# Masked attention over a sparse graph: attention's steps begin earlier, and one tile is transposed onto another in PSUM

## The chip, the cores and the metric

The kernel runs on one core of a Trainium2 chip. The metric is the time of one execution on the device in microseconds (us); three runs of the kernel before gave 635.58, 635.72 and 637.35, median 635.72. The engines go by the profile's names: PE (TensorE, matrix products; PEld is its weight load), DVE (VectorE), ACT (ScalarE), POOL (GpSimd) and SP (SyncE, which here only issues DMAs). [...]

## The reference

With x of 2708 x 1024 and adj of 2708 x 2708, which holds a 1 with a chance of 0.0014771 and a 0 otherwise (some four edges in a row):

```python
h = jnp.maximum(_layernorm(x, axis=-1), 0.0)
q = h @ W_q.T + b_q
k = h @ W_k.T + b_k
v = h @ W_v.T + b_v
z = scale * (q @ k.T)                     # scale = 1 / sqrt(1024)
spare_z = z * adj
spare_z = jnp.where(spare_z == 0.0, -10000.0, spare_z)
out = softmax(spare_z, axis=1) @ v
x = x + relu(out)
```

## The kernel before

**The algebra.** M = scale W_q^T W_k is formed once. q stands for h M (so that a score is q of a row times h of its neighbour), and the weighted sum of neighbours' h rows is multiplied by W_v at the end. Only rows that adj marks are ever read: the kernel searches adj for the edges, sorts the rows by their number of edges, and works on tiles of 128 rows of like number. Tile t has K[t] slots; for the tiles that matter here K is 3, 3, 4, 5, 5 for tiles 6, 5, 4, 3, 2, then 7 for tile 21 (the second part of the longest rows), 8 for tile 0, 1 for tile 20, 2 for 7, 3 for 17, 5 for 13, 3 for 18. Tile 20 has no scores. This is also attention's order.

**Units.** The products run in 20 units of two tiles each. Units 0 to 9 make q of tiles (0, 1) to (18, 19); units 10 to 19 make the outputs, in attention's order: (6, 5), (4, 3), (2, 0), (20, 7), (17, 13) and so on. Each unit multiplies a 2 x 2 arrangement of blocks in seven block products instead of eight (Strassen's way, Winograd's form): the first tile's halves are a11 and a12, the second tile's are a21 and a22, and four sums are formed of them by `blocks`:

s1 = a21 + a22, s2 = s1 - a11, s3 = a11 - a21, s4 = a12 - s2.

`multiply` issues the products in this order: Y s2, X a12, Z s4, Y s3, then of the next unit X a11 and Z s1 (`opened`, called by `between`), then Y a22. Each is four matrix products of 128 x 128 by 128 x 512, which are eight instructions in the profile (line 1010). X, Z and Y are banks of PSUM; the next unit's banks take over those that have been read. Between the products stand the points `after(0)` to `after(6)`: `after(i)` says what the other engines do at that place. The results leave by c11, c12, c22 and c21: c12 (line 1094, DVE) after Z s4; c22 (line 1091, DVE) after Y s3; c21 (line 1099, ACT) after Y a22. Bank Y is added into again by Y a22 after c22 has read it. In units 4 and 5 (`EARLY <= ta < EARLY + 4`) and in the output units ACT copies Y for c22 first; in the other q units DVE reads Y itself.

**Operands.** Rows of a tile are turned by PE (`half_turned`, line 415: four transposes into one bank of PSUM) and copied out by ACT (line 718), or, where a tile was finished early enough ("faced"), they are stored in quarters and turned by DVE (line 705). `upper` makes a11 and a12, `lower` makes a22 and the sums. In most units `upper` is at point 0 and `lower` at point 2 of the unit before; where `turn` is set (units 0 and 3) they are at points 3 to 5.

**Attention** is a generator, `stream`, of small steps: a score is one DVE instruction over 128 x 1024 (line 863, `junk`), counted as 1.3 us; the weights of a tile count 0.6; each further slot's sum is one DVE instruction (line 923, `u`), counted as 1.3. `advance(share)` at each point takes out steps until `share` us are spent; `share` is 20.9/7 (21.5/7 in the last units), less 2.3/7 for each faced row of the next unit. DVE's order is the written one from start to end (`manual_schedule`); the order of ACT and POOL is written in units 0 to 3 and chosen by the compiler's scheduler after that, as PE's and SP's is. A tile's scores need `pq`, its q rows in sorted order: for tiles under 8 a gather from q_dram, for the others a plain load from q_late (line 833, issued by POOL), which unit (t / 2) has stored through SP (line 1084). They need `g`, the neighbours' rows, gathered by POOL into eleven buffers (line 610).

**Before attention** come the search for edges (`found`, line 389), the list of each row's neighbours (`listed`, lines 402 to 408), `counts` (lines 661 to 669), `sort` (lines 678 to 689, two small products on PE), the scatter of the table into DRAM (`put`, line 626), its `reload` (line 638), and the clearing of the buffers g (line 1262). The list `steps_at` says at which (unit, point) each runs, and `steps_ahead` what runs ahead of the rest of a point: `"i21"` finds tile number 21 of the search, `"j21"` lists it, `"c0"` counts and `"o0"` sorts the first half of the rows, `"w0-7"` scatters, `"b0"` reloads.

**Places that the change touches**: `blocks` (line 718 and after), `steps_at` and `steps_ahead`, `opened`, the loop over units with `share`, the memsets (line 1262), `advance`, and the place where `load_rows` fetches the rows of the unit after next (line 612 for q's).

Of the kernel before, what the change touches and what calls it, by code (L numbers as in the profile page):

```python
# [10 lines left out]
FT = mybir.dt.float32  # L11
# [4 lines left out]
ALU = mybir.AluOpType  # L16
AX = mybir.AxisListType

P = 128
# [46 lines left out]
def tile_preln_masked_attention(  # L66
# [12 lines left out]
    nc = tc.nc  # L79
# [28 lines left out]
    psum = ctx.enter_context(tc.tile_pool(name="psum", bufs=4, space=bass.MemoryType.PSUM))  # L108
# [13 lines left out]
    ident = const.tile([P, P], FT, name="ident")  # L122
# [70 lines left out]
    first = const.tile([P, PARTS, 8], FT, name="first")  # L193
# [216 lines left out]
    def half_turned(xt, s):  # L410
# [4 lines left out]
            nc.tensor.transpose(pt[:, c, :], xt[:, k * P:(k + 1) * P], ident)  # L415
        return pt

    def turned(xt, name):

        hT = work.tile([P, D], FT, tag="hT", name=f"T_{name}", bufs=2).rearrange("p (c q) -> p c q", q=P)  # L420
        for s in range(DC // 4):
            nc.scalar.copy(hT[:, s * 4:(s + 1) * 4, :], half_turned(xt, s))
        return hT
# [7 lines left out]
    tp = low.enter_context(tc.tile_pool(name="tp", bufs=1, side="left", reuse_waits="tile"))  # L431
# [14 lines left out]
    with tc.tile_pool(name="w", bufs=1, side="left") as wp:  # L446
# [73 lines left out]
        if True:  # L520
# [13 lines left out]
            for o in range(DC):  # L534
# [4 lines left out]
                else:  # L539
                    k = o - H  # L540
# [61 lines left out]
    half = low.enter_context(tc.tile_pool(name="half", bufs=1, side="left", reuse_waits="tile"))  # L602
# [11 lines left out]
    rows_of = {}  # L614
    FIRST = EARLY // 2
# [6 lines left out]
    def put(lo, hi):  # L622

        before_them = puts[lo >= EARLY]
        for t, (t0, n) in tiles_of(lo, hi):
            put = nc.gpsimd.indirect_dma_start(  # L626
                out=tab_dram[lo >= EARLY][:, :], out_offset=bass.IndirectOffsetOnAxis(ap=pos_i[:n, t:t + 1], axis=0),
                in_=tab[:n, t, :], in_offset=None)
            for other in before_them:
                tc.declare_no_dep(put.ins, other.ins, reason="rows of a permutation")  # L630
            before_them.append(put)
        return put
# [75 lines left out]
    def is_faced(xt):  # L708
        return any(xt is y for y in faced)

    def blocks(xa, xb, eng=None):


        ops = {}

        def held(name, bank):
            ops[name] = small(name).rearrange("p (c q) -> p c q", q=P)
            nc.scalar.copy(ops[name], bank)

        def put(name, a, b, op, eng=None):  # L720
            ops[name] = small(name).rearrange("p (c q) -> p c q", q=P)
            step = (eng or nc.vector).tensor_tensor(ops[name], a, b, op=op)  # L722
            if eng is None:
                behind.append(step)

        def faced_half(name, xt, s):
            ops[name] = small(name).rearrange("p (c q) -> p c q", q=P)
            faces(ops[name], xt, s * 4, s * 4 + 4)

        def upper():  # L730
            for s, name in enumerate(("a11", "a12")):
                if is_faced(xa):
                    faced_half(name, xa, s)
                else:
                    held(name, half_turned(xa, s))

        def lower():
            if is_faced(xb):
                faced_half("a22", xb, 1)
                faced_half("s3", xb, 0)  # L740
                put("s1", ops["a22"], ops["s3"], ALU.add)
                behind.append(nc.vector.tensor_sub(ops["s3"], ops["a11"], ops["s3"]))
            else:
                held("a22", half_turned(xb, 1))
                a21 = half_turned(xb, 0)
                put("s1", ops["a22"], a21, ALU.add)
                put("s3", ops["a11"], a21, ALU.subtract)
            put("s2", ops["s1"], ops["a11"], ALU.subtract, eng)
            put("s4", ops["a12"], ops["s2"], ALU.subtract, eng)

        return ops, upper, lower

    placed = []

# [8 lines left out]
    def natural_rows(n):  # L763
# [3 lines left out]
    ops_of = {0: blocks(*rows_of.pop(0))}  # L767
# [19 lines left out]
    steps_ahead = {(1, 5): "o1", (3, 6): "o0"}  # L787

    slots, free = [], []

# [217 lines left out]
    def add_block(bank, a, b, last=True):  # L1008
        for c in range(4):
            mm = nc.tensor.matmul(bank, a[:, c, :], b[:, c, :], start=False, stop=(c == 3), skip_group_check=True)  # L1010
        return mm
# [3 lines left out]
    def opened(n):  # L1015

        if n not in banks_of:
            return
        X, Z = banks_of[n]
        ops = ops_of[n][0]  # L1020
        add_block(X, ops["a11"], M[:, 0, 0])
        Y = psum.tile([P, NB], FT, tag="acc", name="psy")
        nc.scalar.copy(Y, X)
        products.append(add_block(Z, ops["s1"], T[:, 0] if units[n][0] == "q" else M[:, 0, 1]))
        p5 = small("p5")
        nc.scalar.copy(p5, Z)
        opened_of[n] = Y, p5
# [203 lines left out]
    for n, unit in enumerate(units):  # L1231
# [5 lines left out]
            nc.sync.dma_start(bp_dram, bp_sb[0:1, :])  # L1237
        turn = n in (0, FIRST - 1)
        share = (20.9 if n < len(units) - 5 else 21.5) / 7
        nxt = units[n + 1] if n + 1 < len(units) else None  # L1240
        if nxt is not None and nxt[0] == "o":
            share -= 2.3 / 7 * len(set(nxt[1:]) & faced_tiles)
# [2 lines left out]
        def after(i):  # L1245
# [4 lines left out]
            if (n, i) == (2, 5):  # L1250
# [5 lines left out]
                owe(7)  # L1256
                rows_of[FIRST + 1] = load_rows(units[FIRST + 1])
                pooled.close()
            if n == FIRST and i in (1, 4, 5):
                for g in slots[:4] if i == 1 else slots[4:6] if i == 4 else slots[6:8]:  # L1260
                    with tc.issue_after(sorted_at[-1].ins):
                        nc.vector.memset(g, 0.0)
            b11, t1, b21, b22 = M[:, 0, 0], M[:, 0, 1], M[:, 1, 0], M[:, 1, 1]
# [24 lines left out]
                marked(EARLY, NT)  # L1288
            if (n, i) == (FIRST + 2, 4):
                nc.vector.tensor_scalar(msq, msq, MLIMIT, None, op0=ALU.is_gt)  # L1290
            if n > FIRST + 1 or n == FIRST + 1 and i > 1:
                advance(share)
            if nxt is not None:

                if i == (3 if n == 0 else 4 if turn else 0):
                    ops_of[n + 1] = blocks(*rows_of[n + 1], nc.gpsimd if n + 1 < FIRST - 1 else None)
                    with tc.issue_after(products[-1].ins) if n + 1 == FIRST else nullcontext():
                        ops_of[n + 1][1]()
                if i == (4 if n == 0 else 5 if turn else 2):
                    ops_of[n + 1][2]()  # L1300
                    rows_of.pop(n + 1)
                    if n == last_q - 1:
                        all_rows()
                if i == 3:
                    banks_of[n + 1] = banks_for(bp_sb)
                if i == 6 and n + 2 < FIRST:
                    natural_rows(n + 2)
                if i == (2 if n == FIRST else 3 if n == last_q else 4) and n + 2 > FIRST and n + 2 < len(units) and n + 2 not in rows_of:
                    while units[n + 2][0] == "o" and not done.issuperset(units[n + 2][1:]):
                        advance(1.0)  # L1310
                    rows_of[n + 2] = load_rows(units[n + 2])
# [259 lines left out]
```

## Time and profile before

| what | value |
|---|---|
| median of three runs | 635.72 us (635.58 to 637.35) |
| the profiled execution's own time | 631.83 us |
| its span, first to last instruction | 630.1 us |
| PE busy | 619.6 us (98%) |
| DVE busy | 523.3 us (83%) |
| ACT busy | 288.4 us (46%) |
| POOL busy | 363.1 us (58%) |
| granted clock of PE, mean | 0.999 |
| DMA | 182.19 MB, mean 289 GB/s |

The times in a row of a timeline are the start from the beginning of the span and the duration, both in us; in brackets stands how long the engine was idle before it and what ended that. In a row of the waits stand the total, the number and the longest. In a row of the chain of waits stand start and duration. In a row of groups stand count, busy time and mean ns of one, then the idle time before them. DVE and ACT instructions overlap by some 0.1 us from one to the next.

### The profile page before, as it was taken

How to read it: one execution, taken by the hardware profiler on the slowest of the kernel's cores; microseconds unless marked ns; L12 is line 12 of the kernel's file. 1: busy time of each engine (PE TensorE's matmuls, PEld its weight loads, DVE VectorE, ACT ScalarE, POOL GpSimd, SP SyncE). 2: the span in 40 equal slices, each digit the busy share in tenths (PEclk: the TensorE clock that was granted, in tenths of full speed). 3: DMA queues.
4: the chain of work that ended last, by engine and by line, in shares of the span. 5: the costliest groups of instructions: out<-in, count | busy, mean ns of one | idle time of the engine just before them, and what ended most of it. 6: DMA issues, size and time to landing. Idle time of an engine off the chain costs nothing.

```text
span 630.1 us, 6067 instructions
## 1 busy us (share of the span) xinstructions
PE 619.6 (98%) x1579; PEld 310.3 (49%) x1579; DVE 523.3 (83%) x1022; ACT 288.4 (46%) x421; POOL 363.1 (58%) x394
## 2 busy tenths in 40 slices
PE   8999999999999999999999998999999999999996
PEld 5777766444444444454454443444444444444442
DVE  5999879997996664887988969999997999988741
ACT  3538985749677563343341333434342323343300
POOL 2649860885778177754561632757667477852241
PEclk9999999999999999999999999999999999999999
DMA  8999997688796439997489998899999999997481
GB/s 330 407 371 326 343 354 294 209 288 326 255 387 241 166 113 319 350 379 236 154 306 325 332 359 265 235 333 346 347 318 324 344 278 305 349 284 194 103 296 71
DMA packets 65088, 182.19 MB, mean 289 GB/s; under 512 B 9959, under 2 KB 20023, under 8 KB 64408
## 3 DMA queue, kind: packets, MB, share of 16 engines
q0 software_dynamic: 26656, 86.02, 43.4%
q1 hardware_dynamic: 31594, 71.53, 32.8%
q10 hardware_dynamic: 6798, 24.20, 9.8%
q8 instruction: 14, 0.23, 0.2%
q14 instruction: 26, 0.21, 0.1%
HBM read 146.70 MB, written 43.36 MB: 302 GB/s over the span
## 4 chain that ended last, share of the span: by engine, by line
PE 56%; DMA 17%; DVE 11%; issue 9%; POOL 4%; ACT 1%; SPq 1%; POOLq 0%; DVEq 0%; ACTq 0%
PE ps L1010 22%; PE psy L1010 15%; PE ps_y L476 7%; DMA out_dram<-y,tab 5%; PE ps_x L476 4%; DMA or<-u_dram 4%; PE ps_z L476 4%; DVE junk L863 4%; PE pt L415 3%; DMA pq<-q_late 2%; DVE u L923 2%; DMA q_late<-q 2%; DMA g<-h_dram,tab 2%; DMA u_dram<-v 1%; DVE a L705 1%
## 5 line engine op out<-in xcount | busy, mean ns | idle before, releaser
L1010 PE MATMUL psy<-wlow,s 128*128 128x512 f32 x320 | 144.0, 592 | 0.0
L1010 PE MATMUL ps<-M,a 128*128 128x512 f32 x320 | 144.0, 593 | 0.0
L610 POOL DMA_INDIRECT g<-h_dram,tab x91 | 110.3, 1212 | 55.8 <-ACT u L912 19.8
L863 DVE SCALAR_TENSOR_TENSOR junk<-g,pq 128x1024 uint8<-128x1024 f32 x90 | 110.0, 1223 | 16.8 <-DMA g<-h_dram,tab 10.2
L1010 PE MATMUL ps<-M,s 128*128 128x512 f32 x240 | 108.0, 592 | 2.2 <-DVE s L722 2.2
L1010 PEld LDWEIGHTS psy<-wlow,s 128*128 128x128 f32 x320 | 59.9, 190 | 72.4 <-issue 70.2
L1010 PEld LDWEIGHTS ps<-M,a 128*128 128x128 f32 x320 | 59.9, 190 | 71.8 <-issue 71.3
L923 DVE SCALAR_TENSOR_TENSOR u<-g,coef,u 128x1024 f32<-128x1024 f32 x66 | 84.6, 1282 | 4.9 <-ACT u L912 3.5
L1010 PEld LDWEIGHTS ps<-M,s 128*128 128x128 f32 x240 | 45.4, 190 | 59.7 <-issue 58.3
L389 DVE FIND_INDEX8 at<-ones,adj 128x8 uint32<-128x685 f32 (+1 forms) x88 | 74.5, 865 | 0.0
L1010 PE MATMUL psy<-wlow,a 128*128 128x512 f32 x160 | 72.0, 593 | 0.1
L368 ACT ACTIVATE sized<-adj 128x2708 uint8<-128x2708 f32 (+1 forms) x22 | 54.3, 2466 | 7.5 <-DMA adj<-in_adj_dram 6.1
L298 POOL TENSOR_TENSOR hsum<-hsum,x 128x256 f32<-128x256 f32 (+1 forms) x56 | 38.7, 728 | 25.4 <-DVE wlow L444 22.0
L1109 POOL DMA_INDIRECT y<-in_x_dram,tab x19 | 32.2, 1696 | 31.4 <-ACT y L1126 22.4
L1010 PEld LDWEIGHTS psy<-wlow,a 128*128 128x128 f32 x160 | 30.3, 190 | 38.7 <-issue 37.3
L944 ACT COPY v<-u 128x1024 f32<-128x1024 f32 x19 | 19.9, 1045 | 48.9 <-DVE u L923 43.5
L808 POOL DMA_INDIRECT out_dram<-y,tab x21 | 27.8, 1325 | 22.0 <-issue 13.6
L1010 PE MATMUL ps<-wlow,s 128*128 128x512 f32 x80 | 36.0, 592 | 0.0
L626 POOL DMA_INDIRECT tab_dram<-tab,pos_i x22 | 21.9, 993 | 20.9 <-DVE pos_i L689 15.4
L912 ACT ACTIVATE u<-g,coef 128x1024 f32<-128x1024 f32 x18 | 20.7, 1148 | 24.2 <-DVE coef L911 24.1
L760 ACT COPY ps<-bp_sb 128x512 f32<-128x512 f32 x42 | 24.6, 595 | 11.0 <-DVE y L1144 10.3
L276 ACT ACTIVATE x<-x,r 128x1024 f32<-128x1024 f32 (+1 forms) x22 | 25.8, 1232 | 5.6 <-POOL r L266 5.6
(251 smaller groups left out, 848.5 us busy)
## 6 DMA issues: line engine op xcount, KB each, us to landing
adj<-in_adj_dram SPq DMA_DIRECT2D x21, 1354.0 KB, 11.2
x<-in_x_dram SPq DMA_DIRECT2D x21, 512.0 KB, 4.2
h_dram<-x ACTq DMA_DIRECT2D x21, 512.0 KB, 8.4
u_dram<-v ACTq DMA_DIRECT2D x19, 512.0 KB, 8.5
or<-u_dram SPq DMA_DIRECT2D x76, 128.0 KB, 9.7
q_late<-q SPq DMA_DIRECT2D x12, 512.0 KB, 9.4
pq<-q_late POOLq DMA_DIRECT2D x12, 512.0 KB, 10.5
M<-in_wv_dram SPq DMA_DIRECT2D x3, 1024.0 KB, 15.4
```

Of the source, the lines that this page charges most:

```text
L276: nc.scalar.activation(xs[i][:n], xs[i][:n], AF.Relu, bias=r[:n, 4, i:i + 1], scale=r[:n, 3, i:i + 1])
L298: small.append(nc.gpsimd.tensor_add(hsum[:n, cols], hsum[:n, cols], xt[:n, cols]))
L368: nc.scalar.activation(sized[:n], a[:n, :, :PW], AF.Abs, accum_out=total[:n, t:t + 1])
L389: nc.vector.max_index(at[:n, k - first_k, g, :], ones[:n, 0:8], a[:n, g, :])
L476: mm = nc.tensor.matmul(bank, a_tile(o + H * a[0], a[1], i), b(o), start=first and o == 0, stop=(o == H - 1), skip_group_check=True)
L610: return nc.gpsimd.indirect_dma_start(out=dst, out_offset=None, in_=src, in_offset=off, bounds_check=N - 1, oob_is_err=False)
L760: nc.scalar.copy(return_[h], row[:, h * NB:(h + 1) * NB])
L808: to = nc.gpsimd.indirect_dma_start(out=out, out_offset=bass.IndirectOffsetOnAxis(ap=ptab.bitcast(U32)[:n, t, SLOTS:SLOTS + 1], axis=0), i ...
L863: chained(lambda: nc.vector.scalar_tensor_tensor(junk, g_of[t][s], 1.0, tq[t], op0=ALU.mult, op1=ALU.mult, accum_out=zall[:, t, s:s + 1]))
L923: chained(lambda: nc.vector.scalar_tensor_tensor(u, g_of[t][s], coef[:, s:s + 1], u, op0=ALU.mult, op1=ALU.add))
L1010: mm = nc.tensor.matmul(bank, a[:, c, :], b[:, c, :], start=False, stop=(c == 3), skip_group_check=True)
L1109: return nc.gpsimd.indirect_dma_start(out=y[:n], out_offset=None, in_=x, in_offset=off, compute_op=ALU.add)
```

## The change

It has five parts.

1. `"j21 c0"` (list and count) moves from point 5 to point 4 of unit 3, and the sort, `"o0"`, from point 6 of unit 3 into `opened`, between unit 4's first two products.
2. The eight memsets of g, which stood at points 1, 4 and 5 of unit 4, all stand at point 1.
3. `advance` begins at point 0 of unit 5, no longer at point 2, and `share` is less by 2.3/7 in unit 9 and by 4.6/7 in unit 10.
4. The q rows for units 7, 8 and 9 are gathered at point 2 of units 5, 6 and 7, no longer at point 4.
5. For units 3 and 5 and after, where the second tile isn't faced, a new step at point 1, `middle`, transposes its upper half (a22) into a bank, from which ACT copies it; at point 2 the lower half (a21) is transposed onto the same bank, so that PE forms s1 = a22 + a21 there and ACT copies s1. DVE makes s2 = s1 - a11, s3 = a22 - s2 and s4, and no longer s1. Units 1, 2 and 4 stay as they were.

```diff
+    def turn_onto(pt, xt, s, first):
+
+        for c in range(4):
+            k = s * 4 + c
+            nc.tensor.matmul(pt[:, c, :], xt[:, k * P:(k + 1) * P], ident, is_transpose=True, start=first and c == 0,
+                             stop=(c == 3), skip_group_check=True)
...
-    def blocks(xa, xb, eng=None):
+    def blocks(xa, xb, eng=None, onto=False):
...
+        half = []
+
+        def middle():
+            if onto and not is_faced(xb):
+                half.append(psum.tile([P, 4, P], FT, tag="tp", name="pt"))
+                turn_onto(half[0], xb, 1, True)
+                held("a22", half[0])
+
         def lower():
             if is_faced(xb):
...
-            else:
+                put("s2", ops["s1"], ops["a11"], ALU.subtract, eng)
+            elif not onto:
                 held("a22", half_turned(xb, 1))
                 a21 = half_turned(xb, 0)
                 put("s1", ops["a22"], a21, ALU.add)
                 put("s3", ops["a11"], a21, ALU.subtract)
-            put("s2", ops["s1"], ops["a11"], ALU.subtract, eng)
+                put("s2", ops["s1"], ops["a11"], ALU.subtract, eng)
+            else:
+                turn_onto(half[0], xb, 0, False)
+                held("s1", half[0])
+                put("s2", ops["s1"], ops["a11"], ALU.subtract)
+                put("s3", ops["a22"], ops["s2"], ALU.subtract)
             put("s4", ops["a12"], ops["s2"], ALU.subtract, eng)
...
-                (3, 1): "i21", (3, 3): "p21", (3, 5): "j21 c0 g0", (3, 6): "w0-7 g1 g2 g3 g4", (4, 4): "b0"}
-    steps_ahead = {(1, 5): "o1", (3, 6): "o0"}
+                (3, 1): "i21", (3, 3): "p21", (3, 4): "j21 c0", (3, 5): "g0", (3, 6): "w0-7 g1 g2 g3 g4", (4, 4): "b0"}
+    steps_ahead = {(1, 5): "o1"}
...
         Y = psum.tile([P, NB], FT, tag="acc", name="psy")
         nc.scalar.copy(Y, X)
+        if n == FIRST:
+            follow("o0")
         products.append(add_block(Z, ops["s1"], T[:, 0] if units[n][0] == "q" else M[:, 0, 1]))
...
+        if n in (last_q, last_q + 1):
+            share -= 2.3 / 7 * (n - last_q + 1)
...
-            if n == FIRST and i in (1, 4, 5):
-                for g in slots[:4] if i == 1 else slots[4:6] if i == 4 else slots[6:8]:
+            if n == FIRST and i == 1:
+                for g in slots[:8]:
                     with tc.issue_after(sorted_at[-1].ins):
                         nc.vector.memset(g, 0.0)
...
-            if n > FIRST + 1 or n == FIRST + 1 and i > 1:
+            if n > FIRST:
                 advance(share)
...
-                    ops_of[n + 1] = blocks(*rows_of[n + 1], nc.gpsimd if n + 1 < FIRST - 1 else None)
+                    ops_of[n + 1] = blocks(*rows_of[n + 1], nc.gpsimd if n + 1 < FIRST - 1 else None, n > 1 and not turn)
...
+                if i == 1 and not turn:
+                    ops_of[n + 1][3]()
...
-                if i == (2 if n == FIRST else 3 if n == last_q else 4) and n + 2 > FIRST and n + 2 < len(units) and n + 2 not in rows_of:
+                if i == (2 if FIRST <= n <= last_q - 2 else 3 if n == last_q else 4) and n + 2 > FIRST and n + 2 < len(units) and n + 2 not in rows_of:
```

Here FIRST is 4 and last_q is 9.

More of the change, by code (lines that the diff above doesn't have):

```diff
@@ L747, in lower @@
                 put("s3", ops["a11"], a21, ALU.subtract)
-            put("s2", ops["s1"], ops["a11"], ALU.subtract, eng)
+                put("s2", ops["s1"], ops["a11"], ALU.subtract, eng)
[4 more added lines that the diff above has]
+                put("s3", ops["a22"], ops["s2"], ALU.subtract)
             put("s4", ops["a12"], ops["s2"], ALU.subtract, eng)
-        return ops, upper, lower
+        return ops, upper, lower, middle
     placed = []
```

## The prediction

> **What bounds the kernel now.** I read the page's head first, then the waits of PE, then PE's timeline where the longest wait lies, then the chain of waits and the timelines of DVE and POOL behind it.
>
> ```profile
> span 630.1 us, 6067 instructions
> PE 619.6 (98%) x1579; PEld 310.3 (49%) x1579; DVE 523.3 (83%) x1022; ACT 288.4 (46%) x421; POOL 363.1 (58%) x394
> ...
> PE ps L1010 <- DVE s L722: 2.2, 1, 2.2
> PE ps_y L511 <- POOL hsum L121: 1.2, 1, 1.2
> PE ps L1010 <- DVE T_alone L705: 0.8, 1, 0.8
> PE ps_x L476 <- DMA wlow<-in_wq_dram: 0.6, 1, 0.6
> ```
>
> TensorE is the bound: busy 619.6 of 630.1 us. All its waits on record come to 4.8 us, and 2.6 of these lie at the start and the end, which the change doesn't touch. No product or transpose is removed, so the most that can be gained is the one wait of 2.2 us. What can be lost has no such limit: the change moves work on DVE, whose order is written out by hand, and PE waits for DVE at some places. Here is the wait:
>
> ```profile
> 360.65 3.60 PE L1010 MATMUL ps<-M,a 128*128 128x512 f32 x8
> 364.08 3.60 PE L1010 MATMUL ps<-M,s 128*128 128x512 f32 x8
> 367.52 3.60 PE L1010 MATMUL psy<-wlow,a 128*128 128x512 f32 x8
> ...
> 384.68 3.60 PE L1010 MATMUL ps<-M,a 128*128 128x512 f32 x8
> 390.44 3.67 PE L1010 MATMUL ps<-M,s 128*128 128x512 f32 x8 [2.16 <-DVE s L722]
> ```
>
> A block of eight rows is 3.43 us (start to start). Unit 9 (tiles 18 and 19, the last of q) ends with the block at 367.52; unit 10 follows, and inside it unit 11's second product (390.44) waited 2.16 us for its operand s1. DVE before that:
>
> ```profile
> 365.73 0.68 DVE L1091 TENSOR_TENSOR q<-psy,p 128x512 f32<-128x512 f32 x1
> 366.33 1.22 DVE L863 SCALAR_TENSOR_TENSOR junk<-g,pq 128x1024 uint8<-128x1024 f32 x1
> ...
> 367.47 1.28 DVE L923 SCALAR_TENSOR_TENSOR u<-g,coef,u 128x1024 f32<-128x1024 f32 x1
> 372.38 1.23 DVE L863 SCALAR_TENSOR_TENSOR junk<-g,pq 128x1024 uint8<-128x1024 f32 x1 [3.64 <-DMA pq<-q_late]
> ...
> 373.65 1.23 DVE L863 SCALAR_TENSOR_TENSOR junk<-g,pq 128x1024 uint8<-128x1024 f32 x1
> ...
> 389.60 0.69 DVE L722 TENSOR_TENSOR s<-a,s 128x512 f32<-128x512 f32 x1
> ```
>
> DVE ran late by itself and then stood 3.64 us for the q rows of attention's tile 17. The chain of waits says where these come from:
>
> ```profile
> 347.73 10.06 DMA q_late<-q
> ...
> 358.32 13.95 DMA pq<-q_late
> ```
>
> q of tile 17 is the last result of unit 8. It is stored when that unit ends (347.73), lands at 357.79, is read back by POOL from 358.32 and is there at 372.27. These two times are set by PE's progress and by DMA, not by how early attention begins.
>
> **The change, part by part.**
>
> *Keys, sort, memsets (unit 3 and 4).*
>
> ```profile
> 208.76 0.28 DVE L402 TENSOR_TENSOR cand<-first,at 128x128 f32<-128x128 f32 x1
> ...
> 205.18 0.69 DVE L1091 TENSOR_TENSOR q<-psy,p 128x512 f32<-128x512 f32 x1 [3.56 <-PE psy L1010]
> ...
> 213.27 0.22 DVE L669 TENSOR_SCALAR tab<-keys 128x128 uint32<-128x128 f32 x1
> 216.48 0.31 DVE L682 COPY sort<-ps_all 128x144 f32<-128x144 f32 x1 [2.99 <-PE ps_all L680]
> ...
> 240.75 1.23 DVE L863 SCALAR_TENSOR_TENSOR junk<-g,pq 128x1024 uint8<-128x1024 f32 x1 [5.17 <-DMA g<-h_dram,tab]
> ...
> L1262 DVE MEMSET g<- 128x1024 f32 x8 | 7.3, 912 | 1.3 <-issue 1.3
> 209.28 3.60 PE L1010 MATMUL ps<-wlow,s 128*128 128x512 f32 x8
> ```
>
> The listing and counting (208.76 to 213.5, 4.7 us) moves one point up, ahead of the addition at 205.18, where DVE stood idle 3.56 us. So unit 4's additions slip by about 1 us; their s1, due on PE at 209.28, is ready near 207.7. The two products of the sort go between two blocks, before 209.28 instead of after 216.15 (two blocks earlier, 6.9 us). The table's scatters, its reload and the first gathers follow on POOL and SP in the same order, so the first score moves from 240.75 to about 233.9. Eight memsets in one row cost (7.3 + 1.3) 8.6 us of DVE, from about 212.2 to 220.8, and unit 5's additions start at 224.7. Nothing of this reaches PE: cost 0; without the 3.56 us of idle time 1 to 3 us would.
>
> *Attention steps.* Each of a unit's seven points (0 to 6) takes 20.9/7 = 2.99 us of steps. After the change unit 5 gives seven points instead of five, and units 9 and 10 lose 2.3 and 4.6 us. I count where the first score of tile 17 falls, since that is the step that waits. The steps ahead of it are 37 scores (tiles 6, 5, 4, 3, 2, 21, 0, 7 with 3, 3, 4, 5, 5, 7, 8, 2 slots) and 30 sums at 1.3, and eight weights at 0.6: 91.9 us. It runs at the first point where more than 91.9 has been given out. Before: 26 points of 2.99 in units 5 to 8 are 77.6, and unit 9 gives 16.3/7 = 2.33 each (its next unit has two faced rows: 20.9 - 4.6), so 91.6 at point 5 and 94.0 at point 6: point 6, as the trace shows (two scores from 372.38, after the addition of 365.73). After: 28 points are 83.6, unit 9 gives (20.9 - 4.6 - 2.3)/7 = 2.0: 91.6 at point 3, 93.6 at point 4. So it moves to **point 4, ahead of the addition c22 of unit 9** (the row at 365.73). That addition reads PE's bank Y in place (only tiles 8 to 11 have it copied by ACT first), and the block of 367.52 adds into the same bank, so PE can't start it before c22 has read. c22 now queues behind two scores that wait for the q rows of tile 17.
>
> With landing time L, c22 ends at L + 3.2: from the landing at 372.27 the second score ended at 374.88, and c22 takes 0.68 more. PE's wait is L + 3.2 - 367.5 = L - 364.3. DVE was there at 368.7 before (372.38 less 3.64); now it has c22 and five additions of 0.68 less ahead, and its steps, 4.6 us more of them by then, began 6.9 sooner: it will be there some 6 us earlier, ahead of L. c22's own input is ready at 360.65. The old wait of 2.16 us goes: between L and s1 stand the 17.9 us of before (372.38 to 390.29) and 2.5 us more (c22, one score, one weights), so s1 is ready at L + 20.4, while PE, late by L - 364.3, wants it at 388.3 + L - 364.3 = L + 24.
>
> What is L? Rows of the store (L1084) and of the read (L833), each least, median, longest, and two single reads:
>
> ```profile
> DMA to landing us min/median/max: 2.6/7.9/12.2
> ...
> DMA to landing us min/median/max: 6.5/10.5/16.4
> ...
> pq<-q_late POOLq DMA_DIRECT2D x1, 512.0 KB, 8.4
> ...
> 352.88 1.49 POOL L610 DMA_INDIRECT g<-h_dram,tab  x1 [0.30 <-issue]
> 358.32 0.57 POOL L833 DMA_DIRECT2D pq<-q_late  x1 [3.95 <-DMA q_late<-q]
> ```
>
> POOL had stood 3.95 us for the store, so the read can't be issued sooner unless the store lands sooner. I keep the store at 10.06 and take the median 10.5 for the read rather than its own 13.95: the gathers that ran up to 352.88 ahead of it are asked for some 6 us sooner and should be further through. L = 358.3 + 10.5 = 368.8; wait 4.5 us. Low end: store 7.9, 0.5 to issue, read 8.4 (that of 380.26, no gather close ahead): L = 364.5, wait 0.2. High end: the longest read, 16.4: L = 374.7, wait 10.4.
>
> [...]
>
> *a21 onto a22 in PSUM.*
>
> ```profile
> L722 DVE TENSOR_TENSOR s<-a,s x26: 691/692/693, 108.0 to 583.9; 128x512 f32<-128x512 f32 x26
> L722 DVE TENSOR_TENSOR s<-a,pt x24: 670/680/689, 106.1 to 555.1; 128x512 f32<-128x512 f32 x24
> ...
> L718 ACT COPY a<-pt x32: 564/590/619, 104.5 to 549.2; 128x512 f32<-128x512 f32 x32
> ...
> 521.24 1.04 PE L415 MATMUL pt<-ident,u 128*128 128x128 f32 x8
> ...
> 522.40 1.04 ACT L944 COPY v<-u 128x1024 f32<-128x1024 f32 x1 [3.72 <-DVE u L923]
> ...
> 526.44 0.57 ACT L718 COPY a<-pt 128x512 f32<-128x512 f32 x1
> ```
>
> It applies to eight units (3, 5 to 9, and the two output units with an untransposed second tile). DVE loses one addition of 0.68 each (5.4 us, none on PE's path but where DVE is late), ACT gains one copy of 0.59 each (it is 46% busy). PE has the same eight transposes, but four come a block earlier, and the last four may not begin before ACT has copied a22 out of that bank. That is a new wait of PE on ACT, with one block (3.43 us) of cover. ACT stands for DVE now and then: at 522.40 it had waited 3.72, and a22's copy ended at 527.0. Were it to stay at that place, PE, which wants it near 521.7, would wait 5.3 us; if ACT takes it before v, nothing. In q's units the copies of the first tile came early enough. I take 0, since the copy is now issued a block sooner, and keep 5.3 as the end.
>
> *q rows sooner.* Six gathers on POOL, some 1.3 us each with their issue, move two blocks up in units 5 to 7; POOL is 58% busy and the score gathers behind them belong to steps that are 6 us ahead: 0. SP gets nothing new. If POOL's order let the gathers of tile 13 past the read of tile 17, that would count to L's high end.
>
> **Sum.** 631.8 (the profiled execution's own time, span 630.1) - 2.16 + 4.5 = 634.2, or +2.3 us. The runs' median is 635.7, 3.9 above the profiled time; I add the difference to it: **638.0 us**, 0.37% slower. About 0.3% (1.9 us) is what a measurement of this kernel can tell from no change.
>
> **Rivals.**
> - *The q rows land in time* (the ending on the other side). With L at 364.5 or less c22 isn't held, and the old wait is gone: -2.2 us, 633.6. For it: the read of 8.4 us, and gathers that leave the queue sooner. Against it: store and read together took 24.5 us and must take under 16.8 (347.73 to 364.5). It decides at L = 366.5, where old and new wait are equal.
> - *ACT's copy of a22 holds PE too*, at the late output units: with the forecast's wait and half of 5.3 on top, +5.0, 640.7. For it: ACT's waits for DVE stand just there. Against it: ACT's order is chosen by readiness, and the copy is ready early.
> - *The wait stays where it was.* If DVE reaches these scores so late, or the order comes out so, that c22 isn't held and s1 is still late: 0, 635.7. Against it: DVE's order in the trace is the written one everywhere I compared.
>
> **How the numbers follow.** Forecast (PE held before the last block of unit 9 by 2.2 to 8 us): 0.50, with times from 635.7 to 641.5. Rows in time: 0.27. ACT's copy: 0.13. No shift: 0.10. Slower by over 0.3%: the part of the forecast with L above 368.4 (0.32) and ACT's (0.12): 0.44. Faster by over 0.3%: nearly all of the second case, 0.24, as its gain is just over that bound. Within: the rest, 0.32. The range from 633.3 to 642.0 reaches from the in-time case to the read of 13.95.
>
> **What would show it.** Right: on DVE the first score of tile 17 stands ahead of unit 9's L1091 addition, with a wait for pq<-q_late; PE waits for that addition before the psy<-wlow,a block near 367.5; no wait for s1 in unit 10; the first score near 234. Wrong: PE without a wait there (L was early), PE waiting for ACT's copies of a22, or the score behind the addition.

## The result, and the profile after

The changed kernel takes 640.3 us (median of ten runs, 637.9 to 648.5) against 636.4 us for the kernel before (median of ten): a ratio of 1.0065, with a 95% interval of 1.0043 to 1.0088. It is slower by about 4 us. The ratios and intervals of this document leave out executions more than 1.5% above the fastest of their kernel, such as the one of 648.5. Its profiled execution has a span of 640.6 us and a time of 642.3. The profiled execution of the kernel before (631.8) is shorter than all its other executions on this chip (634.3 and more in these ten, 633.2 and more in all), so the two spans are 10.5 us apart where the medians differ by 3.9. On a second chip, which comes up below, the kernel before takes 630.9 to 634.5, and which chip the first trace comes from isn't known. The traces are read below for places, and the ratios for sizes.

The head of the page after:

```profile
span 640.6 us, 6061 instructions
PE 624.8 (98%) x1579; PEld 312.2 (49%) x1579; DVE 522.4 (82%) x1014; ACT 294.1 (46%) x429; POOL 365.0 (57%) x394
```

TensorE is busy for 5.2 us more with the same 1579 instructions: some of them ran slower. The rest is waits. What PE waited for, after (line and tile, releaser: total, times, longest):

```profile
PE pt L422 <- ACT a L725: 3.3, 1, 3.3
PE ps L1031 <- ACT ps L781: 2.9, 1, 2.9
PE ps L1031 <- DMA M<-in_wv_dram: 1.6, 1, 1.6
PE ps_y L518 <- POOL hsum L121: 1.2, 1, 1.2
PE ps L1031 <- DVE q L1114: 0.9, 1, 0.9
PE psy L1031 <- DVE q L1114: 0.4, 1, 0.4
```

The old wait for s1 in unit 10 (2.2) and the small one near the end (0.8) are gone. Five new ones have come. The two large ones are for ScalarE, at the transposes of a21 onto a22 and at the copies that open a unit's banks. A unit's operands are made in the unit before: the wait in unit 2 (183.11 below) belongs to the transposes for unit 3, the one in unit 5 (256.30) to those for unit 6. PE's timeline at the four places of interest (start, duration, line, tile, count, idle time and releaser); "..." separates units 2, 5 and 9:

```profile
172.70 0.60 PE L422 MATMUL pt<-ident,x 128*128 128x128 f32 x4
176.57 3.60 PE L1031 MATMUL psy<-wlow,s 128*128 128x512 f32 x8
183.11 5.40 PE L1031 MATMUL ps<-M,a 128*128 128x512 f32 x8 [2.94 <-ACT ps L781]
...
249.36 3.60 PE L1031 MATMUL psy<-wlow,s 128*128 128x512 f32 x8
256.30 1.12 PE L422 MATMUL pt<-ident,qr 128*128 128x128 f32 x4 [3.34 <-ACT a L725]
257.21 5.92 PE L1031 MATMUL ps<-M,a 128*128 128x512 f32 x8
...
374.66 3.67 PE L1031 MATMUL ps<-M,a 128*128 128x512 f32 x8 [1.56 <-DMA M<-in_wv_dram]
382.13 3.70 PE L1031 MATMUL psy<-wlow,a 128*128 128x512 f32 x8 [0.36 <-DVE q L1114]
```

Behind each of the two long waits a block takes 5.4 and 5.9 us where 3.6 is usual. A view in windows shows the granted clock around unit 5 (columns: window, length, busy time and count of PE, PEld, DVE, ACT, POOL, then the clock, the DMA share and GB/s):

```profile
248.00:280.00 32.00, 28.66 (x73) 13.51 (x72) 22.35 (x43) 12.01 (x19) 18.90 (x17) 0.89 0.95 313
```

The clock is 0.89 over these 32 us. With the transposes (1.12 for 0.60) and the block (5.92 for 3.60) the wait of 3.34 us costs 6.2.

Why does ScalarE come late? Its timeline in unit 2, and then in unit 5 ("remote": what released it isn't in the profile):

```profile
168.18 1.54 ACT L725 COPY a<-pt 128x512 f32<-128x512 f32 x3
174.65 0.59 ACT L1077 COPY u<-psy 128x512 f32<-128x512 f32 x1 [4.93 <-PE pt L422]
179.05 0.59 ACT L725 COPY s<-pt 128x512 f32<-128x512 f32 x1 [3.82 <-remote]
179.54 2.47 ACT L368 ACTIVATE sized<-adj 128x2708 uint8<-128x2708 f32 x1
181.99 0.58 ACT L1111 COPY q<-ps 128x512 f32<-128x512 f32 x1
182.46 1.12 ACT L781 COPY ps<-bp_sb 128x512 f32<-128x512 f32 x2
...
253.02 1.15 ACT L933 ACTIVATE u<-g,coef 128x1024 f32<-128x1024 f32 x1 [5.63 <-issue]
254.10 0.20 ACT L893 ACTIVATE w<-zall 128x3 f32<-128x3 f32 x1
254.22 0.57 ACT L1122 COPY q<-psy 128x512 f32<-128x512 f32 x1
254.68 1.56 ACT L725 COPY a<-pt 128x512 f32<-128x512 f32 x3
```

*Unit 2.* In this unit ScalarE's order is the written one. The second half of the transposes may begin only when a22 has been copied, and PE does them after a whole block, at 172.70. ScalarE's copy of s1, which needs them, stands in its order ahead of `sized`, of c11 and of the two copies from 182.46 that open unit 3's banks. PE wants the banks at 180.0 (176.57 and a block of 3.43) and gets them at 183.1. In the kernel before, the copy in this place was a22's, which needed no other copy first. The banks were open by 175 there:

```profile
169.66 0.60 ACT L718 COPY a<-pt 128x512 f32<-128x512 f32 x1
...
173.88 1.11 ACT L760 COPY ps<-bp_sb 128x512 f32<-128x512 f32 x2
```

But the order alone doesn't make the wait. PE's second half was done by 173.3 (172.70 and 0.60), but ScalarE began the copy of s1 at 179.05, after 3.82 us for which the profile names no releaser. Such late starts are in the traces from the first chip: c11 is copied between 178.5 and 182.0 in seven of the nine, and in the other two (a21 onto a22 alone, and the changed kernel with c22 copied) TensorE gets the banks, which ScalarE copies after c11, at 183.77 and 183.45. In the first trace of the kernel before and in the four from the second chip c11 is copied by 176.9. (By its times the changed kernel ran on the first.) So the fairer comparison is the kernel without a21 onto a22 (below) on the first chip, where the bank copies start just in time, 3.4 us sooner than after:

```profile
179.02 1.11 ACT L781 COPY ps<-bp_sb 128x512 f32<-128x512 f32 x2
```

What the late starts come from is open (see the last experiment).

*Unit 5.* The three copies from 254.68 are a11, a12 and a22. They stand behind attention's product u (253.02) and its w, which wait for scores on VectorE. The factor of u is ready there only at 252.9:

```profile
252.71 0.23 DVE L932 TENSOR_SCALAR coef<-w,m 128x3 f32<-128x3 f32 x1
```

PE wants a22's bank back at 252.8 (249.36 and 3.43) and gets it at 256.2. One block of cover (3.43 us) isn't enough here: the three copies had their inputs by 249.5, when PE's transposes for them ended (248.93 and 0.60), but ScalarE stood idle for 5.63 us and took u first, as the order in the program has it.

*Unit 9* went as the prediction had it, but a load stands in front. VectorE, and the two DMA pieces of the chain of waits that lead to it:

```profile
360.01 6.66 DMA q_late<-q
367.77 12.31 DMA pq<-q_late
```

```profile
378.97 1.23 DVE L884 SCALAR_TENSOR_TENSOR junk<-g,pq 128x1024 uint8<-128x1024 f32 x1 [3.19 <-DMA pq<-q_late]
380.24 1.23 DVE L884 SCALAR_TENSOR_TENSOR junk<-g,pq 128x1024 uint8<-128x1024 f32 x1
381.39 0.69 DVE L1114 TENSOR_TENSOR q<-psy,p 128x512 f32<-128x512 f32 x1
```

The two scores of tile 17 wait for its q rows, and c22 (381.39) is behind them. It holds PE for 0.36 us only, because PE had lost 1.56 us just before, to a load of v's weights. SyncE's queue says why that load is late (first the kernel before, then after):

```profile
340.25 0.33 SPq L1267 DMA_DIRECT2D M<-in_wv_dram  x1
347.73 0.32 SPq L1084 DMA_DIRECT2D q_late<-q  x1
```

```profile
360.01 0.34 SPq L1107 DMA_DIRECT2D q_late<-q  x1
...
361.12 5.47 SPq L1292 DMA_DIRECT2D M<-in_wv_dram  x2
```

Before, the load was issued ahead of the store of tile 17's q; after, it stands behind it, though the diff doesn't touch these lines. The program's own planner chooses the order of this queue, and parts 1 to 4 of the change altered its choice: with part 5 alone (below) the load is issued at 350.99, ahead of the store at 358.47, and without part 5 it is behind. Which of the four parts does it isn't shown.

### The profile page after: what moved, and what is told of

The parts are those of the page before. It is cut to its first block, busy times and chain, and to the rows that moved or that the text cites. A ratio compares the mean times of both kernels' runs of the same rounds, so it can differ in the third digit from the quotient of the medians.

```text
span 640.6 us, 6061 instructions
## 1 busy us (share of the span) xinstructions
PE 624.8 (98%) x1579; PEld 312.2 (49%) x1579; DVE 522.4 (82%) x1014; ACT 294.1 (46%) x429; POOL 365.0 (57%) x394
## 4 chain that ended last, share of the span: by engine, by line
PE 85%; issue 4%; DMA 4%; POOL 4%; ACT 1%; another core or an unknown queue 1%; DVE 0%; POOLq 0%; SPq 0%
PE ps L1031 39%; PE psy L1031 27%; PE ps_y L483 6%; PE ps_x L483 4%; PE ps_z L483 4%; DMA pq<-q_late 2%; PE pt L415 1%; POOL hsum L298 1%; PE pt L422 1%; DMA q_late<-q 1%; POOL qr L619 1%; POOL tab_dram L633 1%; PE ps_y L518 1%; DMA pq<-q_dram,tab 1%
## 5 line engine op out<-in xcount | busy, mean ns | idle before, releaser
L617 POOL DMA_INDIRECT g<-h_dram,tab x93 | 120.0, 1290 | 69.2 <-ACT u L933 27.6
L1031 PE MATMUL ps<-M,a 128*128 128x512 f32 x320 | 148.3, 607 | 4.5 <-ACT ps L781 2.9
L884 DVE SCALAR_TENSOR_TENSOR junk<-g,pq 128x1024 uint8<-128x1024 f32 x92 | 112.4, 1221 | 9.8 <-issue 3.2
L1031 PEld LDWEIGHTS ps<-M,a 128*128 128x128 f32 x320 | 61.4, 195 | 80.0 <-issue 73.0
L944 DVE SCALAR_TENSOR_TENSOR u<-g,coef,u 128x1024 f32<-128x1024 f32 x70 | 89.7, 1282 | 6.2 <-ACT u L933 4.7
L829 POOL DMA_INDIRECT out_dram<-y,tab x21 | 25.9, 1232 | 23.1 <-issue 13.4
L933 ACT ACTIVATE u<-g,coef 128x1024 f32<-128x1024 f32 x16 | 18.4, 1149 | 21.3 <-DVE coef L932 15.0
```

Source lines behind the costliest of these rows:

```text
L617: return nc.gpsimd.indirect_dma_start(out=dst, out_offset=None, in_=src, in_offset=off, bounds_check=N - 1, oob_is_err=False)
L829: to = nc.gpsimd.indirect_dma_start(out=out, out_offset=bass.IndirectOffsetOnAxis(ap=ptab.bitcast(U32)[:n, t, SLOTS:SLOTS + 1], axis=0), i ...
L884: chained(lambda: nc.vector.scalar_tensor_tensor(junk, g_of[t][s], 1.0, tq[t], op0=ALU.mult, op1=ALU.mult, accum_out=zall[:, t, s:s + 1]))
L944: chained(lambda: nc.vector.scalar_tensor_tensor(u, g_of[t][s], coef[:, s:s + 1], u, op0=ALU.mult, op1=ALU.add))
```

## The experiments

Nine more kernels ran, one of them on both chips, and the kernel before was traced twice more. The two chips differ in their times for the kernel before (636 and 633 us). So the ratio to the kernel before on the same chip counts.

| kernel | median us | before, same chip | ratio | 95% interval |
|---|---|---|---|---|
| changed kernel | 640.3 | 636.4 | 1.0065 | 1.0043 to 1.0088 |
| no a21 onto a22 | 634.4 | 636.4 | 0.9967 | 0.9947 to 0.9986 |
| a21 onto a22 alone | 638.7 | 636.4 | 1.0025 | 1.0002 to 1.0049 |
| onto, without units 3 and 6 | 638.0 | 636.4 | 1.0014 | 0.9991 to 1.0038 |
| onto, in unit 3 only | 632.3 | 633.3 | 0.9987 | 0.9975 to 1.0000 |
| onto, in the output units only | 633.8 | 635.8 | 0.9965 | 0.9942 to 0.9988 |
| onto from unit 4, a point later | 635.8 | 635.8 | 0.9991 | 0.9969 to 1.0012 |
| changed kernel, c22 copied | 640.2 | 636.4 | 1.0056 | 1.0029 to 1.0082 |
| no onto, M loaded sooner | 634.2 | 635.8 | 0.9969 | 0.9944 to 0.9993 |
| the same, and c22 copied | 632.2 | 635.8 | 0.9938 | 0.9913 to 0.9964 |
| the same again, other chip | 629.1 | 633.6 | 0.9943 | 0.9921 to 0.9966 |

**Each half of the change alone.** First the changed kernel without the transposes onto a22:

```diff
-ops_of[n + 1] = blocks(*rows_of[n + 1], ..., n > 1 and not turn)
+ops_of[n + 1] = blocks(*rows_of[n + 1], ..., False)
```

> The changed kernel with a21 never transposed onto a22; keys, sort and attention stay sooner. Theory A (the loss is the new waits of TensorE around ScalarE's copies, in unit 2 at 183 and in unit 5 at 256, and the blocks that run slower behind them): both places go back to what they were, the two waits of 2.9 and 3.3 us and the 1.8 and 2.3 us of slower blocks vanish, and the time is within 1.5 us of the kernel before (635 to 637.5). Theory B (the loss is where attention stands, above all the addition c22 of unit 9, as predicted): the time stays at 639 to 641, with TensorE still waiting for c22 in unit 9.

It is faster than the kernel before, by 0.33% (2.1 us). What its TensorE waited for:

```profile
PE pt L415 <- DMA qr<-h_dram,tab: 2.3, 1, 2.3
PE ps L1031 <- DMA M<-in_wv_dram: 1.7, 1, 1.7
...
PE psy L1031 <- DVE q L1114: 0.3, 1, 0.3
```

Both waits for ScalarE are gone, and unit 9 keeps its two (1.7 and 0.3). Theory A holds, and more: the half of the change for which the prediction saw the loss is a gain. A wait for unit 4's rows (2.3, with 1.7 us of slower work behind it) is new; it comes up again below.

Then the other half by itself, on the kernel before (`turn_onto`, the new `blocks`, and the two calls in the loop over units; nothing else):

> The kernel before with a21 transposed onto a22 in the same eight units, and nothing else of the change. Theory A (the transposes onto a22 cost): unit 2 shows TensorE waiting some 3 us for ScalarE's copies into the banks, as in the changed kernel, since nothing there depends on attention; the time is 2 to 4 us above the kernel before (638.5 to 640.5). Theory B (they cost nothing, as predicted): within 1 us of the kernel before.

0.25% slower (1.6 us), just clear of no change. The places in its trace, which is that of its longest execution (645.1 us) and so is read for places alone:

```profile
183.77 3.70 PE L1031 MATMUL ps<-M,a 128*128 128x512 f32 x8 [3.32 <-ACT ps L781]
...
281.81 1.12 PE L422 MATMUL pt<-ident,qr 128*128 128x128 f32 x4 [3.58 <-ACT a L725]
282.72 4.65 PE L1031 MATMUL ps<-M,a 128*128 128x512 f32 x8
```

The wait of unit 2 is there as expected, again with a late start of ScalarE ahead of it (PE's second half ended at 173.6, 172.97 and 0.60, and ScalarE had begun nothing behind u, 173.90 and 0.59, by 178). The other one is there too, but in unit 6, not 5: it falls where attention's products happen to stand. The halves don't add: the transposes onto a22 cost 1.6 us on the kernel before, and 1.0065/0.9967, some 6 us, where attention runs sooner. Why isn't shown.

**Which units pay.** Three kernels, each the changed kernel with another condition for `onto`:

```diff
-n > 1 and not turn
+n > 3 and n != 5 and not turn    # without units 3 and 6
+n >= last_q                      # the two late output units only
+n == 2                           # unit 3 only
```

> The changed kernel with a21 transposed onto a22 in six of its eight units: units 3 and 6 keep the separate transposes. Theory A (only the copies of these two units hold TensorE): as without any of it, 635 to 637.5, with the waits near 183 and 256 gone. Rival (the wait for ScalarE appears in whichever unit has the a22 copy behind attention's products): one of the units 5, 7, 8 or 9 shows a wait of about 3 us for a transpose or a bank, and the time is 638 to 640.

> The changed kernel with a21 transposed onto a22 in the two late output units only (the edit starts at unit 9, and the units between have a second tile that isn't transposed by TensorE). Theory A (the cost lies in q's units): as without any, 634 to 635.5. Theory B (ScalarE's copies in the late output units hold TensorE, as the prediction's third case had it): 636.5 to 640, and TensorE waits for ScalarE between 500 and 590.

> The changed kernel with a21 transposed onto a22 in unit 3 only. Theory A (in unit 2 the transposes of a21 stand behind the block X a12, ScalarE's written order has the copy of s1 ahead of the copies that open unit 3's banks, and TensorE waits for these): TensorE waits some 3 us for the banks near 183, with slower blocks behind it or not, no other wait for ScalarE, and the time is 2 to 4 us above the kernel without any a21 onto a22 (634.4), 636 to 638. Rival (the units 5 to 9 carry the whole loss, and a wait in unit 2 is won back at unit 4, whose rows then come in time): within 1 us of 634.4, with the wait of 1.4 to 2.3 us for unit 4's rows gone.

The output units cost nothing: 0.9965 beside 0.9967 without any. With units 5, 7, 8 and 9 (and the two free ones) the ratio is 1.0014, half a per cent above no transposes onto a22. So the waits for ScalarE aren't confined to units 3 and 6; theory A of that run falls, and its rival holds in part. In its trace they are short (0.66 and 0.34, in units 6 and 7), and that execution was among the shortest of its twelve (634.2 to 639.0). Unit 3 alone ran on the other chip, where no kernel without it was run: 0.9987, with an interval that ends at no change. There TensorE didn't wait for the banks at all; ScalarE's copies began as soon as their inputs were there:

```profile
173.87 0.58 ACT L725 COPY s<-pt 128x512 f32<-128x512 f32 x1 [3.13 <-PE pt L422]
...
177.27 1.12 ACT L781 COPY ps<-bp_sb 128x512 f32<-128x512 f32 x2
```

So the expected wait near 183 didn't come, and neither theory's time can be judged by this run. What unit 3 costs depends on how late ScalarE starts: its copy of s1 began at 179.05 in the changed kernel, with a wait of 2.94 us behind it, and at 173.87 here, with none. It isn't free even here: unit 4's rows are gathered from 195.42, and TensorE turns them from 203.00 after a wait of 1.7 us. The best version below, the same kernel up to there but for these transposes, turns them from 200.63 on this chip without a wait. The rival had expected that wait to be gone.

**More cover for ScalarE's copy.** Unit 3 keeps the separate transposes, and from unit 4 on the second half is issued one point later, behind the block X a12:

```diff
-ops_of[n + 1] = blocks(..., n > 1 and not turn)
+ops_of[n + 1] = blocks(..., n > 3 and not turn)
...
-if i == (4 if n == 0 else 5 if turn else 2):
+if i == (4 if n == 0 else 5 if turn else 2 if n < FIRST else 3):
     ops_of[n + 1][2]()
```

> The changed kernel with two edits: unit 3 keeps the separate transposes, and from unit 4 on the transposes of a21 onto a22 are issued one point later, after the block X a12, so that ScalarE has two blocks (6.9 us) and not one for its copy of a22. Theory A (TensorE waits for ScalarE's copy of a22, which stands in ScalarE's order behind attention's copies): the waits for that copy in units 5 to 8 vanish and the time is 634 to 636, near the kernel without any a21 onto a22 (634.4). Theory B (the six units' cost is something else: a copy more for ScalarE, another order on VectorE): 638 or more, as with six units (638.0).

0.9991, 635.8 us. In unit 5 ScalarE's a22 copy ends as late as 254.1 behind u, and PE's second half, now behind one block more, goes through at once:

```profile
251.71 3.60 PE L1031 MATMUL ps<-M,a 128*128 128x512 f32 x8
255.14 0.60 PE L422 MATMUL pt<-ident,qr 128*128 128x128 f32 x4
```

No wait for a22 is left in its trace. This carries theory A: the cover was too short, and two blocks are enough. The traces say so more firmly than the times, since the intervals of the two kernels overlap (0.9991 to 1.0038, and 0.9969 to 1.0012). About 0.24% above no transposes onto a22 remain; c22 of unit 9 holds PE for 1.5 us in it (0.3 without), which is part of the rest; that this comes from s2 to s4, which reach VectorE a point later, is only argued.

**The predicted wait in unit 9.** Three kernels. The first is the changed kernel with c22 of unit 9 read from a copy that ScalarE makes, so that the next block needn't wait for VectorE:

```diff
-copied(Y) if EARLY <= ta < EARLY + 4 else Y
+copied(Y) if EARLY <= ta < EARLY + 4 or ta == BARE - 2 else Y
```

> The changed kernel, except that in unit 9 ScalarE copies the bank Y first and the addition c22 reads the copy, as units 4 and 5 have it, so that the last block of unit 9 no longer waits for VectorE. Theory A: the wait for c22 was only 0.4 us, because unit 9 began late; the time moves by less than 1 us (639 to 641), and if unit 9 stands 1.6 us behind the load of M as before, nothing else changes. Theory B (the predicted wait carries the loss): 3 to 4 us less, 636 to 637.

640.2 us, as the changed kernel: theory A. The wait for the load of M was still there (2.00 us) and covered the rest. The two others start from the kernel without transposes onto a22. One issues that load from ScalarE's queue, past the store of q; the other has the copied c22 as well:

```diff
-nc.sync.dma_start(place, src)
+(nc.scalar if at == (0, 0) and place is b11 else nc.sync).dma_start(place, src)
```

> The changed kernel with a21 never transposed onto a22, and the load of the first block of v's weights into M issued by ScalarE's queue, past SyncE's, where it stands behind the store of tile 17's q. Theory A (the predicted wait of unit 9's last block for the addition c22 is there, but the 1.7 us wait for this load covers it): the wait for the load goes, the wait for c22 grows from 0.3 to about 2 us, and the time stays within 0.7 us of 634.4. Theory B (c22 is in time by itself): 1.5 to 2 us less, 632.5 to 633.

> The kernel with the earlier load of M, and c22 of unit 9 read from a copy of its bank that ScalarE makes, so that the last block of unit 9 doesn't wait for VectorE. Theory A: with both waits gone the time falls 1.5 to 2 us below the kernel without a21 onto a22 (634.4), to 632.5 to 633, 0.5% below the kernel before. Theory B (VectorE, late behind the two scores of tile 17, then holds TensorE further on, at s1 of unit 11): 634 to 635, with a wait for s1 in unit 10.

With the load sooner, its wait is gone, and the predicted one comes out in full; the chain of waits, and PE:

```profile
351.19 7.93 DMA q_late<-q
...
359.65 10.54 DMA pq<-q_late
```

```profile
373.37 5.40 PE L1031 MATMUL psy<-wlow,a 128*128 128x512 f32 x8 [2.23 <-DVE q L1114]
```

The time stays (634.2 for 634.4): theory A. With both taken away it falls by 2.0 us to 632.2, a ratio of 0.9938 (the intervals of the two kernels overlap a little), and no wait for s1 takes their place. This version beats both kernels, and did so on the other chip too (0.9943).

**The kernel before, and unit 4's rows.** The kernel before was traced twice more, and the best version once more beside the second of these:

> The kernel before, unchanged, for a second trace of it: its profiled execution (631.8) lay 4 to 5 us under the median of its runs. Theory A (most of its executions have waits that the first trace lacked, such as that for unit 4's rows): TensorE waits 1 to 3 us for the rows near 201, or loses clock behind a wait, and the time is 634 to 638. Theory B (the first trace is typical, and the rest is outside of the span): the same four waits, a span of 630 to 631.

> The kernel with the earlier load of M and with c22 of unit 9 read from a copy, once more, beside a trace of the kernel before taken on the same chip. If the kernel itself makes the rows of unit 4 late, TensorE waits 1 to 2 us for them here again and not in the kernel before; if the chip does, ScalarE starts u2, a22's copy and c11 of unit 2 some 2 us late in both or in neither. Either way the time is 0.4 to 0.8% below the kernel before.

> The kernel before, unchanged, beside the run above: if the late starts of ScalarE in unit 2 (171 to 179) come from the chip, they are here too and TensorE waits for unit 4's rows near 201; if from the changed kernel, ScalarE's copies start at 169 to 174 as in the first two traces, and the only wait over 2 us is that for s1 in unit 10, with a block of 5.4 us behind it in some executions.

Neither trace of the kernel before shows a wait for unit 4's rows. Both show the old wait for s1 of unit 11 in unit 10, longer than in the first trace, and with a block behind it that is 1.7 us too long (here the first of the two):

```profile
391.11 5.37 PE L1010 MATMUL ps<-M,s 128*128 128x512 f32 x8 [2.56 <-DVE s L722]
```

Theory A of the first of them was right about the slower work behind a wait. It was wrong about the rows and about the time: 632.7 us with a span of 630.9, where it had 634 to 638 and theory B a span of 630 to 631. As for the rows: in the kernel without transposes onto a22, on the first chip, ScalarE stood idle 1.6 to 2.3 us ahead of three copies of unit 2 though their inputs were there (it comes first here, then the best version on the second chip):

```profile
171.29 0.58 ACT L1077 COPY u<-psy 128x512 f32<-128x512 f32 x1 [2.34 <-remote]
173.44 0.58 ACT L725 COPY a<-pt 128x512 f32<-128x512 f32 x1 [1.57 <-PE ps L1031]
...
178.54 0.58 ACT L1111 COPY q<-ps 128x512 f32<-128x512 f32 x1 [2.06 <-remote]
```

```profile
169.15 0.60 ACT L1077 COPY u<-psy 128x512 f32<-128x512 f32 x1
169.63 0.61 ACT L725 COPY a<-pt 128x512 f32<-128x512 f32 x1
...
173.37 0.59 ACT L1111 COPY q<-ps 128x512 f32<-128x512 f32 x1 [0.67 <-PE ps L1031]
```

The last two stores of h are issued from 184.91 in the first and from 181.34 in the second, 3.6 us apart, and TensorE turns unit 4's rows from 202.85 and from 200.63. The best version waited 1.4 us for these rows on the first chip and not at all on the second; its only wait of note there is the one at the start. So the late starts go with the chip or the execution, not with the kernel. What they wait for, the profile doesn't say, and whether the kernel before has them on the first chip isn't known: this stays open. The changed kernel itself wasn't run on the second chip, so how much of its 0.65% hangs on these starts isn't known either.

## Why the prediction was right, and where it was wrong

The sign, the range and the likeliest outcome (slower) held: 0.65%, where the forecast said 0.37% (638.0). But the sum came out near the truth through terms that were wrong on both sides, and that is luck. The case to which it gave 0.50, PE held by 2.2 to 8 us before the last block of unit 9, didn't come in the changed kernel: PE was held there for 0.36 us, and the loss came from ScalarE's copies.

- **"It applies to eight units ... I take 0" (a21 onto a22).** This is the step that failed. The transposes onto a22 are the whole loss on the first chip: 1.0% in the changed kernel, against a gain of 0.33% without them. Two premises fell. The cover of one block was counted from PE's side, while ScalarE's queue holds attention's products, which wait for VectorE, ahead of the copy; "the copies of the first tile came early enough" was true, but nobody waits for those until the next unit. And "ACT's order is chosen by readiness" was an assumption about the program's planner; when the program ran, readiness didn't decide, as the rows at 253.02 to 254.68 show: the three copies from 254.68 had their inputs by 249.5 and began behind u, 5.2 us later.
- **ACT's copy as a rival.** The mechanism was named, priced at 5.3 us at most and given 0.13, but put at the late output units, which cost nothing (0.9965). It stood in q's units, 3 and 5 to 9. In unit 3 it is not a22's copy that holds PE but s1's, ahead of the bank copies in a written order; the prediction didn't look at what is queued behind that copy. That wait came out only together with ScalarE's late starts, which no row of the first trace could have shown.
- **The order of VectorE in unit 9, and the wait for c22.** Right in every step: the scores of tile 17 come ahead of c22, and PE waits for c22 before the last block. The size was 2.2 us (with the load out of the way), not 4.5. The term that was too large is L: it fell 19.8 us after unit 9's start (370.20 less 350.4), and 368.8 less 346.9, 21.9, had been forecast, since the store took 7.93 and not 10.06. In the changed kernel the wait was 0.36, because another came first.
- **"SP gets nothing new."** Wrong. Its order changed, and the load of M fell behind the store of q: 1.6 to 2.0 us in every changed kernel that kept it there. It covers the c22 wait, so the two together cost about 2, once.
- **The old wait of 2.16 us.** It vanished, as predicted. It was worth more than its length: in two of three traces the block behind it lost 1.7 us more. So 2.2 to 4.3 us are gained by it, which can pay for unit 9's 2. But none of these traces is known to be from the first chip, where attention's half is faster by 2.1 us, and that kernel loses 4 us at unit 4's rows besides: the 2.1 isn't accounted for in full. Nor is the new place of the scores the only way to lose this wait. It is also gone with a21 onto a22 alone, where they stay behind c22: there the product that reads s1 begins at 398.86 without a wait, right behind the block of 395.43.
- **Keys, sort, memsets.** Right in kind. The first score comes 18.7 us after unit 4 begins (238.84 less 220.12, without transposes onto a22) where it was 24.5 (240.75 less 216.28): 5.8 us sooner, 6.9 predicted. PE waited 0.9 us for an addition in unit 3 of the changed kernel, a cost the step put at 0 and bounded at 1 to 3.
- **"The q rows land in time"**, the ending on the other side, needed L at 17.6 us after unit 9's start (364.5 less 346.9); it was 19.8.

## What to carry to other kernels

When a bank is filled twice, with a copy by another engine in between, count the cover from that engine's queue: what stands ahead of the copy in its order, and what that waits for. Move the second fill behind one block more, or leave the banks separate. And when steps move, look at the issue order of the queues that a planner arranges, even those that the edit doesn't name: a weight load slid behind a store.

## What the hardware showed that was not expected

A stall of TensorE can cost more than its length. After waits of up to 1.9 us (more than a dozen in these fourteen traces from 1.3 on) the next block kept its 3.6 to 3.7 us. Of thirteen waits of 2.0 us and longer, eleven were followed by products and transposes that took 1.6 to 2.8 us more than usual: 2.00, 2.23, 2.56, 2.74 and 2.94 us each by a block of about 5.4; one of 2.16 and one of 3.32 by none. The granted clock goes with it. In the changed kernel it was 0.50 from 183.5 to 186.6 behind the wait of 2.94 and 1.00 from 187.0 on; behind the wait of 3.34 it was 0.50 from 257.2 to 260.6 and 1.00 from 263.0 on. But it was 1.00 from 390.4 to 393.9 behind the wait of 2.16 in the kernel before. An estimate from these windows of unit 3's first block: with 0.83 for 0.4 us, 0.50 for 3.1 us and 0.78 for another 0.4 us, from 183.1 to 187.0, some 1.7 us are lost, which agrees with the 1.8 us that the block took longer (5.40 for 3.60). Which waits bring the clock down isn't settled by their length alone: one of 2.00 was followed by a slow block, and one of 3.32 wasn't.
